# A two-layer Fourier metaformer on one core: the inverse width DFT folded into 64x64 quadrants, the mixed projection tile split into 64-row pairs, and five regimes with their own step orders and PSUM banks

## The chip, the core and the metric

The kernel runs on one NeuronCore of a Trainium2 chip. Its engines run side by side, each through its own queue in program order: TensorE (PE; its weight loads are PEld), VectorE (DVE), ScalarE (ACT), GpSimd (POOL) and SyncE (SP), which here issues all DMAs. The metric is the device time of one execution in microseconds, as the median of several.

## The reference

Eight images of 128 x 128 pixels with 96 channels go through two layers. Each layer is a spectral mixing block and a feed-forward block, both behind a layer norm and added to the residual. Cut to what matters:

```python
# conv block, per layer (x is the normed input, B, H, W, 96)
x_pre = scale * relu(einsum('bhwc,mc->bhwm', x, w1)) ** 2 + bias      # 192 channels
xf    = rfft2(x_pre)                                                 # over H and W
comb  = sum_s filt_s * r[b, s, m]     # three resized filters, weighted by a softmax gate per image
xsp   = irfft2(xf * comb)
y     = einsum('bhwm,cm->bhwc', xsp, w2)                              # back to 96 channels
# feed-forward block, in fp8-e5m2 operands with fp16 rounding of the sums
h = relu(q(x) @ q(W1) + q(b1)); y = q(h) @ q(W2) + q(b2)
```

The gate needs means over a whole image, and each Fourier transform mixes a whole row or column of it.

## The kernel before

The work is cut into three stages, each a Python generator whose `yield` ends a step, and each handles an image in 16 pieces:

- P, `pixels`, takes eight rows of pixels: 0 load xt, 1 norm statistics (DVE), 2 xn (POOL), 3 transposes pt_a (PE), 4 xT (ACT); then for j = 0 and 1: 5/10 projection pw (PE), 6/11 relu r (ACT), 7/12 square xs (ACT), 8/13 acc for the gate (POOL), 9/14 sum and difference sd (DVE); 15 width DFT pa (PE, in 64x64 quadrants), 16/18 lo (ACT), 17/19 at (DVE, L535 and L536), stored to the DRAM buffer a_d.
- F, `frequencies`, takes four width frequencies: 0 load al and ut, 1 ut times the gate (POOL, L626), 2 filter pf (PE, L639, 48-row halves), 3/7 height DFT py (PE, L673), 4 copies cf (ACT, L680), 5/8 products pr (DVE), 6/9 sums xf (POOL, L716), 10/12 projection pz (PE, L747 and L749), 11/13 zt (ACT, L757), 14 inverse height DFT pi (PE, L764), 15 yo (ACT), 16 yt (DVE), stored to y_d. The chunk k = 8 of an image is packed: it holds frequency 0 and 64 together, has a filter part px of its own (L655), adds a constant dc to al (DVE, L628) and clears parts of pr (POOL).
- S, `tokens`, takes eight rows: 0 load v and xr, 1 inverse width DFT ps_r (PE, L793), 2 add to xr (DVE, L802) and statistics, 3/4 norm to fp8 (halves of four rows; DVE L817 or ACT L811, by NORM_ACT), 5 transposes pt_c (PE), 6 xq (ACT, L828), then for k = 0 to 2: 7/11/15 pm (PE, L835), 8/12/16 y16 (ACT, L838), 9/13/17 a16 (DVE, L841), 10/14/18 cast to fp8 (ACT, or POOL in the tail), 19 po (PE), 20 o16 (ACT), 21 add b2 (DVE, L863), 22 residual sum y (POOL, L866) and store.
- N does the small arithmetic of both norms once a tick: 0 variance (DVE), 1 n_rs (ACT, L430 and L431), 2 a correction step and n_nb (DVE). G, the gate of an image, has eleven small steps, which the table GATE puts in front of certain places of TICK in the two ticks after the image's last piece of P.

The order of everything is written out by hand. Time runs in ticks t. In each tick the list TICK is walked, and an entry (stage, step, ahead) issues that step for piece t - offset + ahead. So a larger `ahead` issues a step earlier. F runs 19 ticks behind P and S 40 ticks behind P. Before, three lists are used: RAMP for t < 15 (P alone), TICK from 15 to 275, and TAIL from 276 on (S alone). For t from 15 to 37 S has nothing yet, and from 258 on P has ended, but TICK is used there too. With 16 images-and-layers of 16 pieces there are 256 pieces in each stage.

PSUM is held as four double banks d0 to d3. BANKS names the double bank of each tile, one buffer each: a tile waits until the tile before it on the same double bank has been read.

```python
def bank2(name):
    return pp.tile([128, 2, 512], F32, name=name, tag=f"d{banks[name]}")
```

The SBUF pool `ab` has two buffers for most tiles, three for v, xt and xf, five for xr.

Of the kernel before, what the change touches and what calls it, by code (L numbers as in the profile page):

```python
# [10 lines left out]
F32 = mybir.dt.float32  # L11
# [3 lines left out]
ALU = mybir.AluOpType  # L15
# [5 lines left out]
M = 2 * C  # L21
# [26 lines left out]
NORM_ACT, NORM_ACT_TAIL = (1,), (0, 1)  # L48
CAST_ACT, CAST_ACT_TAIL = (0, 1, 2), ()
XS_ACT = (0, 1)  # L50
# [75 lines left out]
def _constants():  # L126
# [33 lines left out]
    d[32] /= 2  # L160
    rh = np.concatenate([_resize_mat(h, H) for h, _ in SCALES], 1).T
# [35 lines left out]
def metaformer_kernel(ctx: ExitStack, tc: tile.TileContext, x, cst, layers, out):  # L197
# [8 lines left out]
    on_act = {}  # L206
# [61 lines left out]
    def prepare(us, l, p):  # L268
# [114 lines left out]
    def rows(ap, g):  # L383
        return ap.rearrange("w (s h) c -> w s h c", s=2)[:, :, g * RH : (g + 1) * RH, :]
# [7 lines left out]
    class Norms:  # L392
# [13 lines left out]
        def steps(self):  # L406
# [28 lines left out]
            tt(a, a, v, mult)  # L435
            if 1 in self.slots:
                nb = self.nb[:, 1]
                stt(nb, self.sm[:, 1, :, 0], -0.5, self.rs[:, 1], mult, mult)
                stt(nb, self.a[:, 1], 1.5, nb, add, mult)
            stt(rs, a, 1.5, rs, add, mult)  # L440
# [16 lines left out]
    def pixels(jb, g):  # L457
# [26 lines left out]
        for j in range(2):  # L484
# [10 lines left out]
            if j in XS_ACT:  # L495
                nc.scalar.activation(xs, r[:, :, :, :M], AF.Square)
            else:
                pv = pw.rearrange("p a (s c) -> p a s c", c=WE)
                nc.vector.tensor_tensor(xs, pv[:, :, :, :M], r[:, :, :, :M], ALU.mult)
# [9 lines left out]
            nc.vector.tensor_tensor(sd[:, 0], xs[:, 0], xs[:, 1], ALU.add)  # L509
            nc.vector.tensor_tensor(sd[:, 1], xs[:, 0], xs[:, 1], ALU.subtract)  # L510
# [99 lines left out]
    def frequencies(jb, k):  # L610
# [11 lines left out]
        nc.sync.dma_start(ut[:, :KC], ud[:, k0 : k0 + KC])  # L622
        if packed:
            nc.sync.dma_start(ut[:, KC:], ud[:, NKW - 1 :])
        yield
        nc.gpsimd.tensor_tensor(ut[:, :n], ut[:, :n], _bc_mid(jb.rw, n), ALU.mult)  # L626
# [6 lines left out]
        def filter_mm(j):  # L633
            pf = bank2(f"pf{j // 2}")
            for t in range(1 if packed and j == 0 else 0, 3):
                lo = 64 if packed and j == 0 and t == 1 else 0
                c0 = j * M + 128 * t
                for i in range(2):
                    mm(  # L639
                        pf[lo:, i, t * 128 : (t + 1) * 128],  # L640
                        utf[64 * i : 64 * i + NHS, c0 + lo : c0 + 128],
                        kt["rh"][64 * i : 64 * i + NHS, :],
                        start=True,
                        stop=True,
                    )
# [310 lines left out]
```

## Time and profile before

| | us |
|---|---|
| median of 3 runs | 5290.39 (5288.39 to 5291.29) |
| profiled execution, its own time | 5289.91 |
| span in the profile | 5288.1 |
| PE busy | 5025.9 (95%) |
| DVE busy | 4721.0 (89%) |
| ACT busy | 4404.8 (83%) |
| POOL busy | 2627.8 (50%) |
| DMA | 1020.45 MB, 193 GB/s over the span |

The span runs from the first to the last instruction, and the execution's own time is 1.8 us longer. Busy shares are averages over stretches with different limits. The profile can be cut into stretches of time, and the steps of a tick can be read from the timeline. Times in the text such as 3003.89 are us from the span's start. The distance from the start of one instruction to the start of the next on an engine that never idles is called its slot; durations are longer than slots[...].

### The profile page before, as it was taken

How to read it: one execution, taken by the hardware profiler on the slowest of the kernel's cores; microseconds unless marked ns; L12 is line 12 of the kernel's file. 1: busy time of each engine (PE TensorE's matmuls, PEld its weight loads, DVE VectorE, ACT ScalarE, POOL GpSimd, SP SyncE). 2: the span in 40 equal slices, each digit the busy share in tenths (PEclk: the TensorE clock that was granted, in tenths of full speed). 3: DMA queues.
4: the chain of work that ended last, by engine and by line, in shares of the span. 5: the costliest groups of instructions: out<-in, count | busy, mean ns of one | idle time of the engine just before them, and what ended most of it. 6: DMA issues, size and time to landing. Idle time of an engine off the chain costs nothing. (4 is left out here: it accounts for less than half of the span.)

```text
span 5288.1 us, 115779 instructions
## 1 busy us (share of the span) xinstructions
PE 5025.9 (95%) x41160; PEld 3997.8 (76%) x41160; DVE 4721.0 (89%) x13665; ACT 4404.8 (83%) x7147; POOL 2627.8 (50%) x1893
## 2 busy tenths in 40 slices
PE   4889999999999999999999999999999999998876
PEld 1677778788887878788787878878877878877753
DVE  3888889999998999999999999999999999999887
ACT  2745588888898888889898888988888888887778
POOL 0354545555555555555555555555555555554446
PEclk9999999999999999999999999999999999999988
DMA  5466677777777777777777777777777777776544
GB/s 147 162 157 158 169 195 204 205 201 207 205 209 199 204 203 203 204 205 209 201 205 205 206 200 204 211 199 205 205 203 205 206 208 205 198 201 169 165 145 130
DMA packets 908805, 1020.45 MB, mean 193 GB/s; under 512 B 67506, under 2 KB 840722, under 8 KB 907890
## 3 DMA queue, kind: packets, MB, share of 16 engines
q1 hardware_dynamic: 908228, 1013.04, 71.3%
q8 instruction: 327, 5.36, 0.4%
q14 instruction: 250, 2.05, 0.1%
HBM read 598.95 MB, written 413.84 MB: 192 GB/s over the span
## 5 line engine op out<-in xcount | busy, mean ns | idle before, releaser
L716 POOL TENSOR_TENSOR xf<-pr 128x768 f32<-128x768 f32 x512 | 954.8, 1865 | 778.5 <-DVE pr L701 719.8
L505 POOL TENSOR_TENSOR acc<-acc,r 128x192 f32<-128x192 f32 x496 | 338.0, 682 | 1233.3 <-ACT r L492 1224.5
L489 PE MATMUL pw<-w,xT 97*128 97x240 f32 x4096 | 926.1, 370 | 12.8 <-ACT xT L481 12.7
L489 PEld LDWEIGHTS pw<-w,xT 97*128 97x128 f32 x4096 | 763.2, 192 | 124.4 <-ACT xT L481 23.6
L673 PE MATMUL py<-k_fwd,al 128*128 128x128 f32 (+1 forms) x6208 | 832.6, 286 | 0.9
L838 ACT CAST y<-pm 128x1024 f16<-128x1024 f32 x768 | 774.4, 1009 | 41.0 <-PE pm L835 34.2
L673 PEld LDWEIGHTS py<-k_fwd,al 128*128 128x128 f32 (+1 forms) x6208 | 740.8, 194 | 48.4 <-issue 15.4
L845 ACT ACTIVATE h<-a 128x1024 fp8e5<-128x1024 f16 x706 | 747.0, 1058 | 4.7 <-DVE a L841 4.7
L697 DVE TENSOR_TENSOR pr<-py,cf 128x768 f32<-128x768 f32 x512 | 484.9, 947 | 254.4 <-PE py L673 237.0
L817 DVE TENSOR_SCALAR xn_c<-xr,n_rs,n_nb 128x96 fp8e5<-128x96 f32 x948 | 607.8, 700 | 0.0
L626 POOL TENSOR_TENSOR ut<-ut,rw 112x768 f32<-112x768 f32 (+1 forms) x256 | 473.7, 1850 | 242.3 <-DMA ut<-u_d 135.0
L492 ACT ACTIVATE r<-pw 128x960 f32<-128x960 f32 x512 | 492.3, 961 | 100.5 <-PE pw L489 98.5
L747 PE MATMUL pz<-w2b,xf 128*128 128x192 f32 x2048 | 541.8, 346 | 0.5 <-ACT rw L600 0.5
L835 PE MATMUL pm<-xq,f_q 96*128 96x512 fp8e5 x1536 | 465.6, 385 | 16.8 <-ACT zt L757 7.1
L757 ACT COPY zt<-pz 128x384 f32<-128x384 f32 x512 | 244.8, 478 | 271.5 <-PE pz L749 271.5
L747 PEld LDWEIGHTS pz<-w2b,xf 128*128 128x128 f32 x2048 | 329.7, 191 | 180.9 <-issue 142.8
L474 POOL TENSOR_TENSOR xn_a<-xt,n_rs 128x768 f32<-128x768 f32 x256 | 376.5, 1471 | 158.2 <-DMA xt<-in_x_dram 118.3
L639 PEld LDWEIGHTS pf<-k_rh,ut 48*128 48x128 f32 (+1 forms) x6080 | 365.3, 189 | 109.8 <-POOL xf L716 56.4
L793 PE MATMUL ps_r<-v,k_idft 128*128 128x384 f32 x1024 | 401.8, 516 | 41.9 <-DMA v<-y_d 18.2
L639 PE MATMUL pf<-k_rh,ut 48*128 48x128 f32 (+1 forms) x6080 | 419.5, 284 | 22.3 <-POOL ut L626 16.6
L841 DVE TENSOR_SCALAR a<-y,b 128x1024 f16<-128x1024 f16 x768 | 423.3, 551 | 15.2 <-ACT y L838 14.6
L866 POOL TENSOR_TENSOR y<-xr,o 128x768 f32<-128x768 f32 x256 | 425.6, 1662 | 21.7 <-ACT n_rs L431 11.4
(130 smaller groups left out, 10848.5 us busy)
## 6 DMA issues: line engine op xcount, KB each, us to landing
a_d<-at SPq DMA_DIRECT2D x256, 768.0 KB
al<-a_d SPq DMA_DIRECT2D x1024, 192.0 KB
y_d<-yt SPq DMA_DIRECT2D x512, 192.0 KB
v<-y_d SPq DMA_DIRECT2D x256, 384.0 KB
ut<-u_d SPq DMA_DIRECT2D x256, 336.0 KB
xt<-in_x_dram SPq DMA_DIRECT2D x512, 96.0 KB
xr<-in_x_dram SPq DMA_DIRECT2D x128, 384.0 KB
mid<-y SPq DMA_DIRECT2D x128, 384.0 KB
```

The source lines that it names most:

```text
L489: mm(o, xT[:, 4 * a + 2 * i + j, :], wt["w1"], start=True, stop=True)
L492: nc.scalar.activation(r.rearrange("p a s c -> p a (s c)"), pw, AF.Relu)
L626: nc.gpsimd.tensor_tensor(ut[:, :n], ut[:, :n], _bc_mid(jb.rw, n), ALU.mult)
L639: mm(pf[lo:, i, t * 128 : (t + 1) * 128], utf[64 * i : 64 * i + NHS, c0 + lo : c0 + 128], kt["rh"][64 * i : 64 * i + NHS, :], start=True, ...
L673: mm(py[p0:p1, t, e, :], alf[:, e, c0 + p0 : c0 + p1], f, start=True, stop=True)
L697: nc.vector.tensor_tensor(p0, yv, crb, ALU.mult)
L716: nc.gpsimd.tensor_tensor(xf.rearrange("p t e f -> p (t e) f"), pr[:, 0].rearrange("p t r k -> p t (r k)"), pr[:, 1].rearrange("p t r k -> ...
L747: mm(o[:, : 2 * C], xf[:, 1, e, :], wt["w2b"], start=True, stop=False)
L817: nc.vector.tensor_scalar(xn[:, j, :], x8[:, j, :], nm.rs[:, 1, j : j + 1], nm.nb[:, 1, j : j + 1], ALU.mult, ALU.add, saturate=False,)
L835: mm(pm[:, s, :], fk, xq[:, s, :], start=True, stop=True)
L838: nc.scalar.copy(y16, pm)
L845: nc.scalar.activation(hk, a16, AF.Copy, saturate=False)
```

## The change

- **Inverse width DFT.** The matrix `idft` is cut to its first 64 columns. Output pixels w and w + 64 differ only in the sign of the odd frequencies, so even (p = 0) and odd (p = 1) rows are multiplied apart, in four 64x64 quadrants, and VectorE adds both parts to the residual: one add of the even part over 768 elements, then an add and a subtract of the odd part over 384 each. Rows of the residual tiles are laid out anew, so the loads of xr and the stores of y are two DMAs each.
- **Mixed projection tile.** In pz the channel tile 1 holds 64 channels of each of two frequencies. It was multiplied by a 128 x 192 matrix padded with zeros; now its two 64-row halves are multiplied by their own 96 columns, side by side. All four frequencies go to one double bank `pz`, in two steps (the 64-row pairs, then the full tiles), and zt is copied once. F has 16 steps in place of 17: 10 and 11 are pz, 12 zt, 13 pi, 14 yo, 15 yt.
- **Regimes.** RAMP for t < 15, RISE for 15 to 37 (P and F), TICK for 38 to 257, FALL for 258 to 275 (F and S), TAIL from 276, each with its own order and banks. Loads are issued a tick earlier (P 0 ahead 4, F 0 and S 0 ahead 3), and ut is multiplied a tick earlier (F 1 ahead 2).
- **Smaller moves.** In the ramp the second of the two sd operations of each j goes to POOL; in the tail the add of b2 does, and the norm of six rows of eight is on ScalarE (before: all). One of the n_nb operations is gone. In `fft_mm` the loops are turned, and the packed chunk's extra frequency lies first in ut.

The core of the diff. A line of "..." stands for what is left out: the lists GATE, RISE_GATE and TAIL, the old lists, and the index changes of the packed chunk.

```diff
-NORM_ACT, NORM_ACT_TAIL = (1,), (0, 1)
+NORM_ACT, NORM_ACT_TAIL = (4, 5, 6, 7), (0, 1, 3, 4, 5, 7)
 CAST_ACT, CAST_ACT_TAIL = (0, 1, 2), ()
-XS_ACT = (0, 1)
+SD_POOL_RAMP = ((0, 1), (1, 1))
...
 TICK = (
...
+    ("S", 4, 0), ("S", 21, -2), ("P", 10, -1), ("P", 11, -1), ("P", 0, 4), ("F", 2, 1),
+    ("F", 3, 1), ("P", 2, 1), ("P", 1, 2), ("S", 5, 0), ("F", 4, 1), ("P", 12, -1),
+    ("S", 6, 0), ("S", 22, -2), ("S", 1, 1), ("F", 5, 1), ("S", 7, 0), ("S", 14, -1),
+    ("S", 2, 1), ("F", 9, 0), ("P", 3, 1), ("S", 8, 0), ("P", 13, -1), ("S", 15, -1),
+    ("P", 14, -1), ("S", 16, -1), ("N", 0, 0), ("S", 17, -1), ("P", 4, 1), ("S", 9, 0),
+    ("F", 6, 1), ("P", 5, 0), ("N", 1, 0), ("F", 10, 0), ("P", 15, -1), ("F", 11, 0),
+    ("P", 6, 0), ("N", 2, 0), ("F", 7, 1), ("P", 16, -1), ("P", 17, -1), ("P", 18, -1),
+    ("S", 10, 0), ("F", 12, 0), ("S", 0, 3), ("P", 19, -1), ("F", 13, 0), ("S", 11, 0),
+    ("S", 18, -1), ("P", 7, 0), ("F", 8, 1), ("F", 14, 0), ("S", 12, 0), ("P", 8, 0),
+    ("F", 0, 3), ("F", 1, 2), ("F", 15, 0), ("S", 19, -1), ("S", 13, 0), ("S", 3, 1),
+    ("S", 20, -1), ("P", 9, 0),
 )
...
+RISE = (
+    ("P", 1, 2), ("F", 3, 1), ("N", 0, 0), ("F", 4, 1), ("P", 3, 1), ("P", 5, 0),
+    ("F", 10, 0), ("P", 14, -1), ("P", 15, -1), ("P", 0, 3), ("P", 4, 1), ("P", 6, 0),
+    ("F", 5, 1), ("F", 11, 0), ("N", 1, 0), ("P", 16, -1), ("P", 17, -1), ("P", 7, 0),
+    ("P", 8, 0), ("F", 6, 1), ("F", 7, 1), ("F", 1, 2), ("P", 18, -1), ("P", 19, -1),
+    ("F", 12, 0), ("F", 8, 1), ("P", 9, 0), ("N", 2, 0), ("P", 10, 0), ("P", 2, 2),
+    ("P", 11, 0), ("F", 13, 0), ("F", 14, 0), ("F", 0, 3), ("P", 12, 0), ("F", 2, 2),
+    ("F", 15, 0), ("P", 13, 0), ("F", 9, 1),
+)
...
+FALL = (
+    ("S", 14, -1), ("F", 1, 1), ("F", 2, 1), ("F", 3, 1), ("F", 4, 1), ("S", 1, 1),
+    ("S", 21, -3), ("S", 22, -3), ("S", 15, -1), ("S", 4, 0), ("S", 5, 0), ("S", 6, 0),
+    ("F", 9, 0), ("F", 5, 1), ("S", 2, 1), ("F", 6, 1), ("F", 7, 1), ("S", 7, 0),
+    ("S", 8, 0), ("S", 16, -1), ("S", 9, 0), ("F", 10, 0), ("F", 11, 0), ("S", 10, 0),
+    ("F", 12, 0), ("S", 11, 0), ("N", 0, 0), ("S", 17, -1), ("S", 18, -1), ("F", 13, 0),
+    ("S", 19, -1), ("N", 1, 0), ("F", 8, 1), ("N", 2, 0), ("S", 12, 0), ("F", 14, 0),
+    ("S", 13, 0), ("F", 15, 0), ("F", 0, 3), ("S", 3, 1), ("S", 0, 3), ("S", 20, -1),
+)
 RAMP = (
...
+    ("P", 17, -1), ("N", 1, -1), ("P", 2, 2), ("P", 0, 4), ("P", 3, 2), ("P", 18, -1),
+    ("P", 19, -1), ("P", 6, 1), ("P", 12, 0), ("P", 7, 1), ("P", 4, 2), ("P", 1, 4),
+    ("N", 2, -1), ("P", 8, 1), ("P", 13, 0), ("P", 14, 0), ("N", 0, 0), ("P", 9, 1),
+    ("P", 10, 1), ("P", 15, 0), ("P", 11, 1), ("P", 16, 0), ("P", 5, 2),
 )
...
 BANKS = {
...
+    "ps_g": 0, "ph": 1, "pl": 3, "pa0": 2, "pa1": 3, "pw0": 1, "pw1": 1, "pt_a": 3,
+    "pf0": 3, "pf1": 2, "py0": 0, "py1": 1, "pz": 0, "pi": 2, "ps_r": 2, "pt_c": 1,
+    "pm0": 1, "pm1": 3, "pm2": 0, "po": 0, "px": 1, "pg": 0,
+}
...
+    d = d[:, :HH]
...
             stt(a, rs, -0.5, rs, mult, mult)
             tt(a, a, v, mult)
+            stt(rs, a, 1.5, rs, add, mult)
             if 1 in self.slots:
                 nb = self.nb[:, 1]
                 stt(nb, self.sm[:, 1, :, 0], -0.5, self.rs[:, 1], mult, mult)
-                stt(nb, self.a[:, 1], 1.5, nb, add, mult)
-            stt(rs, a, 1.5, rs, add, mult)
...
-            nc.vector.tensor_tensor(sd[:, 0], xs[:, 0], xs[:, 1], ALU.add)
-            nc.vector.tensor_tensor(sd[:, 1], xs[:, 0], xs[:, 1], ALU.subtract)
+            for e, op in enumerate((ALU.add, ALU.subtract)):
+                on = nc.gpsimd if (j, e) in on_pool["sd"] else nc.vector
+                on.tensor_tensor(sd[:, e], xs[:, 0], xs[:, 1], op)
...
-        zt = ab.tile([128, 2, KC * C], F32, name="zt")
-        for j, xf in zip((0, 2), xfs):
-            pz = bank2(f"pz{j // 2}")
+        pz = bank2("pz")[:, :, : 4 * C].rearrange("p t (j e c) -> p t j e c", j=2, e=2)
+        for j, xf in enumerate(xfs):
             for e in range(2):
-                o = pz[:, e, :]
-                mm(o[:, : 2 * C], xf[:, 1, e, :], wt["w2b"], start=True, stop=False)
+                for t in range(2):
+                    q = slice(64 * t, 64 * t + 64)
+                    mm(
+                        pz[:, t, j, e, :], xf[q, 1, e, :], wt["w2b"][q],
+                        start=j == e == 0, stop=False,
+                    )
+        yield
+        for j, xf in enumerate(xfs):
+            for e in range(2):
                 for t in range(2):
                     mm(
-                        o[:, t * C : (t + 1) * C],
-                        xf[:, 2 * t, e, :],
-                        wt["w2c" if t else "w2a"],
-                        start=False,
-                        stop=t == 1,
+                        pz[:, t, j, e, :], xf[:, 2 * t, e, :], wt["w2c" if t else "w2a"],
+                        start=False, stop=j == e == 1,
                     )
...
-        pr = bank2("ps_r")
         for s in range(2):
-            mm(
-                pr[:, s, : RH * C].rearrange("p (h c) -> p h c", c=C),
-                kt["idft"],
-                v[:, :, s, :],
-                start=True,
-                stop=True,
-            )
-        yield
-        xv = xr.rearrange("p s h c -> p s (h c)")
-        nc.vector.tensor_tensor(xv, pr[:, :, : RH * C], xv, ALU.add)
+            nc.sync.dma_start(xr[64 * s : 64 * s + 64], rows(jb.src, g, s))
+        yield
+        pr = bank2("ps_r")[:, :, : RH * C]
+        for p in range(2):
+            for s in range(2):
+                q = slice(64 * p, 64 * p + 64)
+                mm(
+                    pr[64 * s : 64 * s + 64, p].rearrange("p (h c) -> p h c", c=C),
+                    kt["idft"][q],
+                    v[q, :, s, :],
+                    start=True,
+                    stop=True,
+                )
+        yield
+        xv = xr.rearrange("p a h c -> p a (h c)")
+        nc.vector.tensor_tensor(xv, _bc_mid(pr[:, 0], 2), xv, ALU.add)
+        for a, op in enumerate((ALU.add, ALU.subtract)):
+            nc.vector.tensor_tensor(xv[:, a], xv[:, a], pr[:, 1], op)
...
-                if h in on_act["norm"]:
+                if j in on_act["norm"]:
...
-        nc.vector.tensor_tensor(o16, o16, _bc_mid(wt["b2"], RG), ALU.add)
+        on = nc.gpsimd if on_pool["b2"] else nc.vector
+        on.tensor_tensor(o16, o16, _bc_mid(wt["b2"], RG), ALU.add)
...
-        nc.sync.dma_start(rows(jb.dst, g), y)
+        for s in range(2):
+            nc.sync.dma_start(rows(jb.dst, g, s), y[64 * s : 64 * s + 64])
...
             if t < offset["F"] - 4:
-                order, places = RAMP, RAMP_BANKS
-            elif t > n + offset["F"]:
-                order, places = TAIL, TAIL_BANKS
+                order, places, late_steps = RAMP, RAMP_BANKS, {}
+            elif t < offset["S"] - 2:
+                order, places, late_steps = RISE, RISE_BANKS, RISE_GATE
+                on_pool.update(sd=())
+            elif t < n + 2:
+                order, places, late_steps = TICK, BANKS, GATE
+            elif t <= n + offset["F"]:
+                order, places, late_steps = FALL, FALL_BANKS, {}
+            else:
+                order, places, late_steps = TAIL, TAIL_BANKS, {}
                 on_act.update(norm=NORM_ACT_TAIL, cast=CAST_ACT_TAIL)
-            else:
-                order, places = TICK, BANKS
+                on_pool.update(b2=True)
```

## The prediction

> **What bounds the kernel now.** I read the page's first line and engine shares, then the stretches by regime, then the timeline of one steady tick, then single groups.
>
> ```profile
> span 5288.1 us, 115779 instructions
> PE 5025.9 (95%) x41160; PEld 3997.8 (76%) x41160; DVE 4721.0 (89%) x13665; ACT 4404.8 (83%) x7147; POOL 2627.8 (50%) x1893
> ```
>
> ```profile
> 123.00:239.00 116.00, 100.25 (x633) 74.19 (x632) 98.76 (x380) 88.24 (x162) 42.98 (x49) 1.00 0.44 150
> 239.00:611.00 372.00, 330.58 (x2475) 273.18 (x2474) 310.01 (x716) 185.58 (x325) 178.19 (x130) 0.95 0.62 158
> 611.00:4835.00 4224.00, 4189.63 (x35089) 3379.67 (x35089) 3889.18 (x11391) 3750.90 (x5980) 2180.06 (x1557) 0.99 0.76 203
> 4835.00:5126.00 291.00, 243.97 (x1961) 190.66 (x1958) 258.07 (x635) 213.70 (x345) 120.02 (x71) 0.94 0.57 158
> 5126.00:5288.00 162.00, 109.77 (x805) 63.67 (x804) 121.34 (x402) 141.56 (x274) 101.06 (x79) 0.86 0.41 132
> ```
>
> Columns: span, then busy us of PE, PEld, DVE, ACT, POOL, and PE's clock, the DMA share and GB/s. The third row, some 220 ticks with all three stages, has PE busy 99%: there PE's stream is the tick. In rows 2 and 4 (22 ticks without S, 18 without P) PE has 11% and 16% idle, so those ticks (372/22 = 16.9 us, 291/18 = 16.2 us) are set by the order of steps. One steady tick on PE:
>
> ```profile
> 3000.91 1.61 PE L639 MATMUL pf<-k_rh,ut 48*128 48x128 f32 x24
> 3002.45 1.60 PE L673 MATMUL py<-k_fwd,al 128*128 128x128 f32 x12
> 3003.89 0.61 PE L825 MATMUL pt_c<-ident,xn_c 128*96 128x128 fp8e5 x8
> 3004.34 1.51 PE L793 MATMUL ps_r<-v,k_idft 128*128 128x384 f32 x4
> 3005.68 0.60 PE L835 MATMUL pm<-xq,f_q 96*128 96x512 fp8e5 x2
> ...
> 3008.94 1.79 PE L489 MATMUL pw<-w,xT 97*128 97x240 f32 x8
> 3010.66 1.52 PE L519 MATMUL pa<-sd,dft 64*64 64x384 f32 x16
> 3012.11 0.59 PE L747 MATMUL pz<-w2b,xf 128*128 128x192 f32 x2
> ...
> 3019.62 1.61 PE L639 MATMUL pf<-k_rh,ut 48*128 48x128 f32 x24
> ```
>
> Start to start gives slots, and pf to pf the tick: **18.71 us**. Each f32 matmul is two records. ps_r: 4 records, 1.34 us. pa: sixteen 64x64 records with the same 384 columns, 1.45 us, so four quadrants run side by side (about 0.32 us a round of four). VectorE and ScalarE:
>
> ```profile
> L817 DVE TENSOR_SCALAR xn_c<-xr,n_rs,n_nb x728: 314/318/1824, 1213.9 to 4690.5; 128x96 fp8e5<-128x96 f32 x182
> 3003.01 1.48 ACT L680 COPY cf<-pf 128x768 f32<-128x768 f32 x2
> 3004.54 1.02 ACT L828 ACTIVATE xq<-pt_c 96x1024 fp8e5<-96x1024 f32 x1
> 3005.46 0.83 ACT L496 ACTIVATE xs<-r 128x768 f32<-128x768 f32 x1
> ```
>
> L817 has a median of 318 ns and a maximum of 1824. Four in a tick need some 1.0 us and take 2.5: 1.5 us of VectorE is waiting inside them.
>
> [...] in the single records the last pw, with a slot of 0.202, starts at 3010.364, pa at 3010.658, 0.09 us late; the first record after pa has its weight load uncovered, 0.1 us more. [...] 48 rows (pf) 189 ns, 128 rows (py) 194. So 64-row halves cost as many loads, but pf shows them in pairs, 0.112 us a pair. [...] L817: its maximum is one xf of POOL (L716, 1.82 to 1.92 us).
>
> **The change, part by part**, for a steady tick.
>
> *PE.* ps_r goes from 1.35 to two rounds of 0.32, 0.05 for its loads and a drain of 0.09 on either side: 0.88, **-0.47**. pz takes 3.13 us now (1.51 + 1.62). After: eight pairs at 0.112 + 0.1 for the first load + 0.09 drain = 1.08, then sixteen records at 0.1115 (the py pace[...]) + 0.1 = 1.88; 2.96, -0.17. One drain ahead of pz is new, +0.09. PE's sum becomes **18.2 us**, 0.55 under today's tick.
>
> *VectorE.* One add of 0.87 (L802) becomes three: 0.98 with the wait for its own result, 0.47, 0.58: +1.05. One n_nb operation goes (-0.09). L817 gets clean: in the new order POOL has done ut and xn_a when L817 comes, and its y waits for the add of b2 behind L817: -1.5. Sum 16.7 us; now 17.2 (92% of 18.71).
>
> *ScalarE.* Nothing added; its slots make 17.0 us. It had 1.5 us of idle per tick, at 18.2 it has 1.2.
>
> *SP.* xr and y become two DMAs each, 17 issues a tick for 15, loads (P0, S0, F0) a tick earlier. DMA is at 0.76 and SP's queue mostly waits for yt and at (1467 and 877 us), so I take nothing; without that cover, each late load is a PE wait at pf, py or ps_r.
>
> *The new order.* I laid the steps of one tick on the engines with these slots, T = 0 at the end of po. PE: pw1 1.78, pf to 3.32, py0, pt_c and ps_r to 6.09, then pm0. pm0 needs xq. ScalarE: cf can start when pf's last result is there, 3.43; cf 0.68 + 0.69, xs1 0.73 stand ahead of xq in its queue: xq runs 5.53 to 6.55, pm0 starts at 6.60. **PE waits 0.5 us.** From there PE: pm0, pt_a, pm2 1.75, a wait of 0.1 for the bank of pm0 (d1), pw0 1.71, pz 1.08, pa 1.45, pz's rest 1.88, py1 1.34, pi 1.35, pm1 0.44, po 1.02: 12.1. **Tick 18.73.** The gain of PE is given back to a wait on ScalarE. Next in line is VectorE: pr0 can start at 4.9 (py0), three adds, stats and sd1 follow, N0 ends at 11.9; ScalarE's n_rs (N1) stands there from 10.6 on, and behind it r0, lo, a cast and zt, which is still 0.2 us early for pi. Against 18.713, over 206 plain ticks: **+4 us**.
>
> *Per image.* The mean interval of xT (L481) is 19.18, so an image pays 7.5 us beside its 16 x 18.71: the packed chunk and the gate. The dc add (L628, 1166 ns, waiting for POOL) moves to a tick ahead and the gate is spread anew; the px part gets longer in the ScalarE chain (+0.6). I take -1.5 x 13.75 images = **-20** (bounds -50, +15).
>
> *RISE.* Without S, PE's slots are py 2.78, pt_a 0.88, pw 3.4, pz 2.96, pa 1.45, pi 1.36, pf 1.64: 14.5; VectorE 11, ScalarE 8. I find no wait between engines as long as the 0.5 above. 22 x 14.5 + 9 for two gates and a packed chunk = 328 for 372: **-43** (bounds -55, -15).
>
> *FALL.* Slots: PE 12.6, ScalarE 11.8, VectorE 12. Laid out, pf1 waits for po's copy: 13.7, with L817 blocked now and then 14.5, for 16.2: **-30** (bounds -45, 0).
>
> *RAMP.* VectorE 6.4 us of 6.81; two subtractions (0.47 each) go to POOL (4.4 us): about 6.1, x 15: **-10** (bounds -14, +5[...]). *TAIL.* ScalarE 7.5 of some 7.5 to 9; two of eight norms (0.36) go to VectorE, b2 to POOL, v is asked for earlier; but VectorE has +1.05[...]: **-8** (bounds -25, +20).
>
> Sum: +4 - 20 - 43 - 30 - 10 - 8 = **-107**. Profiled execution 5289.91 (0.5 under the median of 5290.39): **5183**.
>
> **Rivals.**
> A, PE stays full. If cf, xs and xq are faster to reach pm0 than I laid out, the tick is 18.2: 206 x -0.55 = -113 more, 5070. For it: today's order leaves PE 1% idle. Against: the 0.5 us wait comes from four durations in a row. 0.2.
> B, VectorE binds, slower. POOL's ut or xn_a falls on L817 again (place: S3, end of the tick). Price: 1.5 us on VectorE, of which 0.7 is free ahead of pr0; 0.8 passes through the three adds, N0 and N1 to zt, 0.2 is slack there: tick 19.35, +130, 5315. It decides from about 1.4 us of blocking a tick on, where +0.5 x 206 eats the 107. For it: 1.5 us today. Against: POOL's queue, with y behind b2. 0.11.
> C, the regimes give little: early ticks are bound by loads or by PE's clock (0.95 in row 2, 0.94 in row 4). RISE and FALL -20 in place of -73: 5236. 0.17.
> D, the quadrants of ps_r do not run side by side: two rounds more, +0.65 us, x 206 = +134: 5317. pa, the same form, speaks against it: 0.02.
> My forecast has 0.5.
>
> **How the numbers follow.** A measurement can tell 0.2% (10.6 us). Forecast, with +-0.25 us on the tick (+-52 us): 5130 to 5240. A lies below, C at its upper end, B and D slower. To leave out 0.2 (half of A, B and D) and to take in the bounds of the parts: **5080 to 5290**. Faster 0.82 (A, the forecast, 0.12 of C), same 0.05 (the rest of C), slower 0.13 (B, D).
>
> **What would show it.** Right: PE busy in the steady row falls to 96 to 97% with pm waiting for xq, L817 at one duration near 318, ps_r near 0.1 us a record, RISE ticks near 14.5. Wrong: steady xT interval under 18.4 (A), L817 still to 1.8 us and ScalarE's n_rs waiting over 2 us (B), pz pairs slower than 0.112.

## The result and the profile after

The changed kernel takes **5158.38 us** (median of 4 runs, 5151.53 to 5159.17) against 5289.39 for the kernel before beside it; ratio 0.9753, 95% interval 0.9736 to 0.977. The profiled execution took 5158.86 us:

```profile
span 5156.8 us, 123945 instructions
PE 4888.7 (95%) x44232; PEld 3746.4 (73%) x44232; DVE 4532.4 (88%) x13904; ACT 4359.2 (85%) x7108; POOL 2608.7 (51%) x1947
```

The shares lie within two points of those before; PE has shed 137 us. The stretches by regime (span, busy us of PE, PEld, DVE, ACT, POOL, PE's clock, DMA share, GB/s) say more:

```profile
121.00:236.70 115.70, 101.36 (x649) 72.06 (x649) 105.95 (x362) 88.81 (x162) 85.46 (x80) 1.00 0.45 153
236.70:551.00 314.30, 305.65 (x2606) 252.02 (x2606) 262.69 (x708) 181.04 (x324) 166.82 (x129) 0.98 0.67 189
551.00:4721.00 4170.00, 4079.31 (x37749) 3171.26 (x37748) 3753.74 (x11616) 3724.20 (x5982) 2101.34 (x1558) 1.00 0.74 206
4721.00:4964.00 243.00, 219.71 (x2102) 165.86 (x2103) 201.26 (x608) 199.52 (x321) 112.54 (x66) 0.97 0.70 183
4964.00:5156.00 192.00, 131.35 (x938) 68.91 (x930) 166.38 (x481) 140.78 (x258) 137.72 (x106) 0.68 0.39 115
```

In the third row PE is 98% busy, not 99%: it waits a little in each tick. In the second it is 97%, where it was 89%. To put the change into parts I took the same marks in both traces: the starts of the same xT pieces (ScalarE, once a tick in P) and yo pieces (once a tick in F), and subtracted.

| stretch, from mark to mark | before | after | change | predicted |
|---|---|---|---|---|
| start and RAMP, to xT piece 17 | 239.25 | 236.74 | -2.5 | -10 |
| RISE, to xT piece 39 | 371.90 | 314.28 | -57.6 | -43 |
| TICK, to yo piece 239 | 4225.45 | 4169.78 | -55.7 | -16 (+4 - 20) |
| FALL, to yo piece 255 | 261.31 | 229.69 | -31.6 | -30 |
| TAIL, to the end | 190.19 | 206.31 | +16.1 | -8 |
| sum | | | -131.3 | -107 |

The plain tick went from 18.713 to 18.638 us. Its PE timeline, where the prediction expected the new wait:

```profile
3002.66 0.61 PE L866 MATMUL pt_c<-ident,xn_c 128*96 128x128 fp8e5 x8
3003.20 0.88 PE L832 MATMUL ps_r<-v,k_idft 64*64 64x384 f32 x8
3004.38 0.59 PE L876 MATMUL pm<-xq,f_q 96*128 96x512 fp8e5 x2 [0.30 <-ACT xq L869]
3004.81 1.04 PE L511 MATMUL pt_a<-ident,xn_a 128*96 128x128 f32 x8
...
3008.05 1.14 PE L776 MATMUL pz<-w2b,xf 64*128 64x96 f32 x16
```

ps_r's slot is 0.88 (1.34 before), and PE then stands 0.30 us for xq. The waits of the steady stretch, PE's first (total us, times, longest), then ScalarE's:

```profile
PE pm L876 <- ACT xq L869: 62.6, 180, 0.8
```

```profile
ACT n_rs L464 <- DVE n_v L462: 268.0, 180, 3.7
```

PE waits 0.35 us a tick for xq; ScalarE stands 1.5 us a tick at n_rs for VectorE. L817 (now L858), which had 314/318/1824 ns, is clean:

```profile
L858 DVE TENSOR_SCALAR xn_c<-xr,n_rs,n_nb x700: 315/322/329, 1202.3 to 4493.0; 128x96 fp8e5<-128x96 f32 x175
```

### The profile page after: what moved, and what is told of

Same layout as the page of the kernel before. It is cut to its first block, busy times and chain, and to the rows that moved or that the text cites. A ratio compares the mean times of both kernels' runs of the same rounds, so it can differ in the third digit from the quotient of the medians.

```text
span 5156.8 us, 123945 instructions
## 1 busy us (share of the span) xinstructions
PE 4888.7 (95%) x44232; PEld 3746.4 (73%) x44232; DVE 4532.4 (88%) x13904; ACT 4359.2 (85%) x7108; POOL 2608.7 (51%) x1947
## 5 line engine op out<-in xcount | busy, mean ns | idle before, releaser
L522 PE MATMUL pw<-w,xT 97*128 97x240 f32 x4096 | 957.6, 377 | 4.2 <-DVE pr L730 2.1
L534 POOL TENSOR_TENSOR acc<-acc,r 128x192 f32<-128x192 f32 x496 | 296.6, 598 | 987.3 <-ACT r L525 928.1
L540 DVE TENSOR_TENSOR sd<-xs 128x384 f32<-128x384 f32 x993 | 508.9, 552 | 4.2 <-ACT xs L528 3.5
L528 ACT ACTIVATE xs<-r 128x768 f32<-128x768 f32 x512 | 438.0, 859 | 0.1
L852 ACT ACTIVATE xn_c<-xr,n_nb,n_rs 128x96 fp8e5<-128x96 f32 x1061 | 407.9, 459 | 31.8 <-DVE n_nb L473 31.8
L668 PEld LDWEIGHTS pf<-k_rh,ut 48*128 48x128 f32 x6080 | 361.7, 188 | 86.2 <-issue 78.5
L668 PE MATMUL pf<-k_rh,ut 48*128 48x128 f32 x6080 | 413.5, 282 | 5.0 <-POOL ut L656 1.8
L784 PE MATMUL pz<-w2a,xf 128*128 128x96 f32 x2048 | 418.1, 286 | 0.0
L784 PEld LDWEIGHTS pz<-w2a,xf 128*128 128x128 f32 x2048 | 312.1, 192 | 144.3 <-issue 142.8
L549 PE MATMUL pa<-sd,dft 64*64 64x384 f32 x4096 | 392.5, 496 | 7.1 <-ACT xT L514 4.5
```

Source lines behind the costliest of these rows:

```text
L522: mm(o, xT[:, 4 * a + 2 * i + j, :], wt["w1"], start=True, stop=True)
L540: on.tensor_tensor(sd[:, e], xs[:, 0], xs[:, 1], op)
L668: mm(pf[:, i, t * 128 : (t + 1) * 128], utf[64 * i : 64 * i + NHS, c0 : c0 + 128], kt["rh"][64 * i : 64 * i + NHS, :], start=True, stop=True,)
L784: mm(pz[:, t, j, e, :], xf[:, 2 * t, e, :], wt["w2c" if t else "w2a"], start=False, stop=j == e == 1,)
```

## Experiments

All edits start from the changed kernel unless it says otherwise. Ratios are to the kernel before, run beside each on the same chip, where it took 5298.74 to 5302.34 us; a tick is the median xT interval in the steady stretch. A digit behind a step's name is its j or k: xs1 is the square of j = 1, y0 the copy y16 of k = 0.

### What the fold is worth

**old_ps_r** puts the unfolded inverse width DFT back; the rest of the change stays.

```diff
-        for p in range(2):
-            for s in range(2):
-                q = slice(64 * p, 64 * p + 64)
...
+        for s in range(2):
...
+                kt["idft"],
+                v[:, :, s, :],
...
-        nc.vector.tensor_tensor(xv, _bc_mid(pr[:, 0], 2), xv, ALU.add)
-        for a, op in enumerate((ALU.add, ALU.subtract)):
-            nc.vector.tensor_tensor(xv[:, a], xv[:, a], pr[:, 1], op)
+        nc.vector.tensor_tensor(xv, pr[:, :, : RH * C], xv, ALU.add)
```

> Changed kernel with the old inverse width DFT (one 128-row matrix, one add of 768, one DMA each for xr and y), all else as changed. Theory: PE's extra 0.47 us fills the wait of pm for xq and the rest of the drains; plain tick 18.65 to 18.75, total 0 to +25 us on the changed kernel: within this order the fold saves almost nothing. Rival (PE's sum sets the tick): 19.1, +100 us.

Measured 5144.19 us, ratio 0.9707 (0.9692 to 0.9721): **faster than the changed kernel**, where the theory had a loss of 0 to 25 us. Its plain tick is 18.635, against 18.638. PE is full for once (second number of the row):

```profile
1300.00:4600.00 3300.00, 3293.40 (x29329) 2590.30 (x29329) 2825.94 (x8909) 3007.09 (x4769) 1674.61 (x1247) 1.00 0.69 207
```

The changed kernel has PE at 3235 us in the same window. So the fold takes 0.33 us of work from PE in each tick (58 us over 177 ticks; ps_r's slot is 0.46 shorter, the slot of pt_c ahead of it 0.09 longer, 0.54 for 0.45, the 0.09 that the prediction calls a drain), and all of it comes back as waiting. Without the fold PE's stream alone is the tick, and it lies 0.08 under the 18.713 of before. That is as much as the prediction gives the pz pairs (-0.17 + 0.09), but no run here undoes the pairs alone. The fold also costs outside the plain ticks: the TAIL tick is 8.58 without it and 8.83 with it.

**fold_alone** is the kernel before with only the fold (matrix, quadrants, adds, DMAs), in the old order and banks. Of its diff, the adds:

```diff
...
-        nc.vector.tensor_tensor(xv, pr[:, :, : RH * C], xv, ALU.add)
+        nc.vector.tensor_tensor(xv, _bc_mid(pr[:, 0], 2), xv, ALU.add)
+        for a, op in enumerate((ALU.add, ALU.subtract)):
+            nc.vector.tensor_tensor(xv[:, a], xv[:, a], pr[:, 1], op)
```

> Kernel before with the folded inverse width DFT alone (64x64 quadrants, three adds, two DMAs each for xr and y), old order and banks. Theory: PE reaches pm 0.47 us earlier, but xq is ready only 0.07 us before pm's present start, so PE waits; VectorE gets 1.05 us more beside L817 still blocked by POOL (17.2 + 1.05 of 18.71): plain tick 18.6 to 19.1, total -20 to +90 us on the kernel before. Rival (PE's sum sets the tick): 18.24, -100 us.

Measured 5589.17 us, ratio 1.0547 (1.0529 to 1.0566), tick 20.37. Both expectations fell; the loss is over three times the larger one. VectorE's timeline in a steady tick, then POOL's:

```profile
3006.79 2.10 DVE L848 TENSOR_SCALAR a<-y,b 128x1024 f16<-128x1024 f16 x1
...
3012.86 2.54 DVE L824 TENSOR_SCALAR xn_c<-xr,n_rs,n_nb 128x96 fp8e5<-128x96 f32 x4
```

```profile
3006.80 1.81 POOL L628 TENSOR_TENSOR ut<-ut,rw 112x768 f32<-112x768 f32 x1
...
3012.69 1.92 POOL L718 TENSOR_TENSOR xf<-pr 128x768 f32<-128x768 f32 x1 [2.47 <-DVE pr L703]
```

a16 takes 2.10 us for 0.47 while POOL does ut, and the four norms 2.54 for 1.04 while it does xf (the norms were blocked as long before). VectorE is busy 3197 of 3300 us: with 0.93 us more of adds (1.91 from the first add to the statistics, for 0.98) and about 3 us of blocked time it is the bound, and PE also waits for its adds, since ps_r and pm0 share a bank in the old table:

```profile
PE pm L842 <- DVE xr L809: 150.0, 167, 1.3
```

So the new TICK order is what makes the fold affordable; the fold makes neither order faster.

**xq_early** moves pt_c, xq and y0 forward in TICK so that pm0 need not wait.

```diff
-    ("F", 3, 1), ("P", 2, 1), ("P", 1, 2), ("S", 5, 0), ("F", 4, 1), ("P", 12, -1),
-    ("S", 6, 0), ("S", 22, -2), ("S", 1, 1), ("F", 5, 1), ("S", 7, 0), ("S", 14, -1),
-    ("S", 2, 1), ("F", 9, 0), ("P", 3, 1), ("S", 8, 0), ("P", 13, -1), ("S", 15, -1),
+    ("S", 5, 0), ("F", 3, 1), ("P", 2, 1), ("P", 1, 2), ("F", 4, 1), ("S", 6, 0),
+    ("P", 12, -1), ("S", 22, -2), ("S", 1, 1), ("F", 5, 1), ("S", 7, 0), ("S", 8, 0),
+    ("S", 14, -1), ("S", 2, 1), ("F", 9, 0), ("P", 3, 1), ("P", 13, -1), ("S", 15, -1),
```

> Changed kernel with three moves in TICK: pt_c (S5) ahead of py0 (F3), xq (S6) ahead of xs1 (P12), y16 of k=0 (S8) ahead of the cast (S14). Theory (two chains): the wait of pm for xq (0.35 us a tick) and of pw0 for y16 (0.1) go, but py0 and with it pr0, the adds, sd1 and N0 come 0.45 us later; n_rs, r0, lo, cast and zt stand behind N0, so pi waits 0.7 us for zt: plain tick 18.9 in place of 18.64, total +50 us on the changed kernel. Rival (the wait at pm is all that PE loses): tick 18.2, total -95 us.

Measured 5249.19 us, ratio 0.9905 (0.9888 to 0.9922), tick 19.06: the theory's direction, with a larger loss than its 18.9. PE does not wait for xq any more; it waits at pi instead:

```profile
PE pi L800 <- ACT zt L791: 63.9, 143, 0.7
```

Two chains hold the tick: cf, xs1, xq to pm0, and py0, the adds, statistics, N0 and n_rs to zt and pi. Shortening the first lengthens the second, since py0 now stands behind pt_c.

**xq_early_r0** is xq_early with r0 ahead of n_rs on ScalarE besides, to fill the wait there.

```diff
-    ("F", 6, 1), ("P", 5, 0), ("N", 1, 0), ("F", 10, 0), ("P", 15, -1), ("F", 11, 0),
-    ("P", 6, 0), ("N", 2, 0), ("F", 7, 1), ("P", 16, -1), ("P", 17, -1), ("P", 18, -1),
+    ("F", 6, 1), ("P", 5, 0), ("P", 6, 0), ("N", 1, 0), ("F", 10, 0), ("P", 15, -1),
+    ("F", 11, 0), ("N", 2, 0), ("F", 7, 1), ("P", 16, -1), ("P", 17, -1), ("P", 18, -1),
```

> The same three moves, and relu r0 (P6) ahead of n_rs (N1) in ScalarE's queue, so that 0.85 us of work no longer stands behind the wait for N0. Theory (two chains): zt is then early enough for pi, PE runs with hardly a wait: plain tick 18.2 (18.15 to 18.35), total -90 us on the changed kernel, 5065 to 5075. Rival (one chain only): no difference between this run and the one without the r0 move.

Measured 5466.27 us, ratio 1.0315 (1.0299 to 1.033), tick 20.06; the theory fell, and so did the rival, which had no difference to xq_early. Two of the five small operations of N0 in VectorE's timeline, and POOL's:

```profile
3016.97 0.50 DVE L460 SCALAR_TENSOR_TENSOR n_v<-n_d 128x16 f32<-128x16 f32 x1
3017.50 1.74 DVE L461 SCALAR_TENSOR_TENSOR n_v<-n_sm,n_v 128x16 f32<-128x16 f32 x1
```

```profile
3016.84 0.59 POOL L534 TENSOR_TENSOR acc<-acc,r 128x192 f32<-128x192 f32 x1 [2.27 <-ACT r L525]
3017.38 1.82 POOL L656 TENSOR_TENSOR ut<-ut,rw 112x768 f32<-112x768 f32 x1
```

r0 releases POOL's acc, and ut follows at once. Both fall on N0, and an operation of 16 elements a partition, 0.17 us when clean, takes 1.74. zt then comes 1.5 us late at pi (200.2 us over 134 ticks).

**xq_early_n0** and **xq_early_n0_zt** start from xq_early and shorten the second chain as well. The diff is that of the first; the second has ("F", 12, 0) ahead of ("P", 6, 0).

```diff
-    ("P", 14, -1), ("S", 16, -1), ("N", 0, 0), ("S", 17, -1), ("P", 4, 1), ("S", 9, 0),
-    ("F", 6, 1), ("P", 5, 0), ("N", 1, 0), ("F", 10, 0), ("P", 15, -1), ("F", 11, 0),
-    ("P", 6, 0), ("N", 2, 0), ("F", 7, 1), ("P", 16, -1), ("P", 17, -1), ("P", 18, -1),
-    ("S", 10, 0), ("F", 12, 0), ("S", 0, 3), ("P", 19, -1), ("F", 13, 0), ("S", 11, 0),
+    ("N", 0, 0), ("S", 16, -1), ("P", 14, -1), ("P", 4, 1), ("N", 1, 0), ("N", 2, 0),
+    ("F", 6, 1), ("P", 5, 0), ("S", 17, -1), ("S", 9, 0), ("F", 10, 0), ("F", 11, 0),
+    ("P", 15, -1), ("P", 6, 0), ("F", 12, 0), ("F", 7, 1), ("P", 16, -1), ("P", 17, -1), ("P", 18, -1),
+    ("S", 10, 0), ("S", 0, 3), ("P", 19, -1), ("F", 13, 0), ("S", 11, 0),
```

> The changed kernel with pt_c, xq and pm0 earlier as in xq_early, and besides: N0 ahead of sd1 on VectorE, n_rs and N2 right behind, pz's rest ahead of pa on PE, zt ahead of lo on ScalarE. Theory (two chains hold the tick, PE waits for xq in the one and ScalarE waits for n_v, then PE for zt, in the other; shorten both and PE's stream of 18.2 us is the tick): plain tick 18.2 to 18.35, some -60 to -90 us on the changed kernel. Rival (r0 comes earlier as N1 does, POOL's acc0 and ut follow at once and fall on the small VectorE operations N2 and on sd1, which are blocked up to 1.8 us as n_v was in xq_early_r0): tick 18.6 to 19.5, 0 to +180 us.

> As xq_early_n0 but with zt ahead of r0 on ScalarE, so that POOL's acc0 and ut start some 0.8 us later, behind N2 and sd1; ScalarE idles some 0.75 us more ahead of zt. Theory of the two chains: tick 18.2 to 18.4 and no blocked n_ operation; -50 to -90 us on the changed kernel. Rival (ScalarE with 16.9 us of work and over 1.3 us of waits becomes the tick): 18.6 to 19.0, 0 to +75 us.

Measured 5461.66 (1.0317, 1.0292 to 1.0343; tick 19.78) and 5248.33 (0.9912, 0.9888 to 0.9936; tick 18.92). Both theories (18.2 to 18.4) fell. In the first the rival came true on another operation, and with a longer tick than it said: not N2 or sd1 but a16, two of them in 2.78 us for 0.88, beside POOL's acc and ut; in this tick pi then waits 1.22 us. VectorE's timeline:

```profile
3000.65 2.78 DVE L882 TENSOR_SCALAR a<-y,b 128x1024 f16<-128x1024 f16 x2
```

In the second nothing is blocked, the tick is the rival's (18.6 to 19.0), and a plain tick has one wait of PE left, 0.37 us at py1 for r0.

**xq_early_banks** takes that wait away by exchanging banks in xq_early_n0_zt.

```diff
-    "ps_g": 0, "ph": 1, "pl": 3, "pa0": 2, "pa1": 3, "pw0": 1, "pw1": 1, "pt_a": 3,
-    "pf0": 3, "pf1": 2, "py0": 0, "py1": 1, "pz": 0, "pi": 2, "ps_r": 2, "pt_c": 1,
-    "pm0": 1, "pm1": 3, "pm2": 0, "po": 0, "px": 1, "pg": 0,
+    "ps_g": 0, "ph": 1, "pl": 3, "pa0": 2, "pa1": 3, "pw0": 1, "pw1": 0, "pt_a": 3,
+    "pf0": 3, "pf1": 2, "py0": 0, "py1": 0, "pz": 0, "pi": 2, "ps_r": 2, "pt_c": 1,
+    "pm0": 1, "pm1": 3, "pm2": 0, "po": 1, "px": 1, "pg": 0,
```

> xq_early_n0_zt with three banks exchanged (py1 and pw1 from bank 1 to 0, po from 0 to 1), so that py1 does not wait for r0 any more. Theory (the wait of 0.37 us at py1 is the only one left on PE, whose slots there add up to 18.55): plain tick 18.55 to 18.65, some 55 to 75 us less than xq_early_n0_zt, level with the changed kernel or up to 20 us under it. Rival (ScalarE, with 16.9 us of work and 2.1 of waits, is the cycle: the wait goes to another place): 18.85 to 19.0, no change on xq_early_n0_zt.

Measured 5343.12 us, ratio 1.0087 (1.0068 to 1.0106). The plain tick stays 18.92, the rival's value: PE now waits 0.36 us at pi for VectorE's `at`, behind it ScalarE's waits of 0.97 at n_rs and 0.75 at zt. The 95 us over xq_early_n0_zt, which neither theory nor rival had, lie in the gate ticks: the two of an image cost 11.4 us beside plain ticks, for 4.6.

### What the regimes are worth

**regimes_off** uses RISE only until F's first piece, and FALL only for the last two ticks.

```diff
-            elif t < offset["S"] - 2:
+            elif t < offset["F"] + 1:
...
-            elif t < n + 2:
+            elif t < n + offset["F"] - 1:
```

> The changed kernel with RISE used only for its first ticks (until the first plane is ready for frequencies) and FALL only for the last two ticks before TAIL; all ticks in between follow TICK. Theory (the regimes' own orders are worth what the ledger shows, some 58 us in the rise and 32 in the fall, of which the common TICK order with its idle stage left out gives a part back): +60 to +85 us on the changed kernel, rise ticks 16.5 to 18, fall ticks 15.5 to 16.5. Rival (an idle stage makes the ticks short in any order, the gain comes from elsewhere): less than +20 us.

Measured 5230.26 us, ratio 0.988 (0.9856 to 0.9903): 67 us more by the profiled spans. Rise ticks are 15.9 for 14.32, and the stretch to xT piece 39 ends 35.6 us later; fall ticks are 15.5 to 18.1 for 14.14, and FALL takes 36.7 more. The theory holds in the sum; rise ticks are shorter than its 16.5 to 18, and some fall ticks longer than its 15.5 to 16.5. TICK with an idle stage is still about a microsecond a tick faster in the rise than the old TICK was, but no faster in FALL (266.4 us for 261.3).

**ramp_tail_on_vectore** gives the ramp's two subtractions and the tail's b2 back to VectorE.

```diff
-SD_POOL_RAMP = ((0, 1), (1, 1))
+SD_POOL_RAMP = ()
...
-                on_pool.update(b2=True)
+                on_pool.update(b2=False)
```

> The changed kernel with the two subtractions of RAMP (SD_POOL_RAMP) and the adds of b2 in TAIL given back from POOL to VectorE; nothing else differs. Theory ([...]what POOL takes over it takes from VectorE's time too): TAIL tick 8.83 to some 8.0 us, n_a (L468, L469) back from 999 and 946 ns to some 170, RAMP tick within -0.5 to +0.2 us; in all -10 to -25 us on the changed kernel. Rival (VectorE is the busy engine there and POOL relieves it): TAIL tick 9.2 to 9.5 us, +7 to +20 us.

Measured 5176.35 us, ratio 0.9779 (0.9752 to 0.9806). My theory fell for both: the ramp tick is 7.86 for 6.86, the TAIL tick 9.30 for 8.83, the rival's figure. In the new orders POOL's help is needed.

**old_ps_r_old_tail** is old_ps_r with the kernel before's TAIL (order, banks, all norms on ScalarE, b2 on VectorE). The two lists are those of the kernel before; beside them:

```diff
-NORM_ACT, NORM_ACT_TAIL = (4, 5, 6, 7), (0, 1, 3, 4, 5, 7)
+NORM_ACT, NORM_ACT_TAIL = (4, 5, 6, 7), (0, 1, 2, 3, 4, 5, 6, 7)
...
-                on_pool.update(b2=True)
+                on_pool.update(b2=False)
```

> old_ps_r (the changed kernel with the unfolded inverse width DFT and one add) with the kernel before's TAIL besides: its step order and banks, all eight norms on ScalarE, b2 on VectorE. Theory (of the 16 us that the tail lost, some 6 are the fold's adds, which old_ps_r gives back, and some 10 come from the new tail order with its norms and b2): the stretch behind the last yo piece 255 falls from 200 us in old_ps_r to 188 to 192, the whole run by 8 to 12 us. Rival (the new tail order is no worse and the loss sits in the hand-over from FALL): 198 to 206 us, no gain or a loss of some 5.

Measured **5128.83** us (5126.85 to 5130.04), ratio 0.9683 (0.9662 to 0.9704): the fastest of all. Behind yo piece 255 it takes 186.4 us, 13.8 less than old_ps_r (200.2), and more than the 8 to 12 of the theory. The loss of 16.1 in TAIL is thus 6.1 for the fold (206.3 - 200.2) and 13.8 for the new tail order with its norms and b2, less 3.8 that comes from elsewhere (190.2 - 186.4). The old tail is the shorter one with the fold too: fold_alone, which has both, takes 201.7 us there, the changed kernel 206.3.

**old_ramp_pool_sd** adds the old RAMP order and banks to that, with the subtractions still on POOL. Its first lines:

```diff
 RAMP = (
-    ("P", 17, -1), ("N", 1, -1), ("P", 2, 2), ("P", 0, 4), ("P", 3, 2), ("P", 18, -1),
+    ("P", 5, 1), ("P", 17, -1), ("P", 18, -1), ("P", 2, 2), ("P", 11, 0), ("N", 1, -1),
...
 RAMP_BANKS = {
-    "pa0": 1, "pa1": 0, "pw0": 3, "pw1": 2, "pt_a": 1,
+    "pa0": 1, "pa1": 3, "pw0": 2, "pw1": 0, "pt_a": 0,
```

> old_ps_r_old_tail with the kernel before's RAMP order and banks besides, but the two subtractions still on POOL. The kernel before has 6.81 us a ramp tick, the changed one 6.86, and the changed one with the subtractions on VectorE 7.86. Theory (what POOL takes over, VectorE gains, as the prediction said; the new order costs what POOL brings): 6.0 to 6.3 us a tick, -8 to -13 us on old_ps_r_old_tail. Rival (1380 ns of POOL and the VectorE operations that it excludes are as long a chain in any order): 6.7 to 7.3 us, -2 to +8 us.

Measured 5158.3 us, ratio 0.974 (0.972 to 0.976). Ramp ticks are 8.1 and 9.4 to 9.8: both expectations fell. POOL does both subtractions behind acc, PE's pa waits for them (14.1 us over 10 ticks), and three of N0's operations are blocked (0.37, 0.85 and 0.92 us, for 0.17). The relief exists only in an order that was laid out for it, and that order with it only equals the old one without it.

### Where an image's 3 us come from

With the xT intervals averaged by their place in the image, an image paid 7.3 us beside plain ticks before (gate 2.9 + 0.2, packed tick 4.1, 0.1 behind it) and pays 4.3 now (1.8 + 0.5, 1.9, 0.1). So 2.2 of the 3 us come from the packed tick and 0.8 from the gate. The old packed tick on PE:

```profile
2522.08 1.26 PE L655 MATMUL px<-k_rh,ut 112*128 112x128 f32 x8 [1.70 <-DVE yt L771]
2523.28 3.51 PE L673 MATMUL py<-k_fwd,al 128*128 128x128 f32 x16
2526.58 0.94 PE L825 MATMUL pt_c<-ident,xn_c 128*96 128x128 fp8e5 x8
2527.36 1.51 PE L793 MATMUL ps_r<-v,k_idft 128*128 128x384 f32 x4
```

px waits for VectorE's yt (they share d2), and in this image py and pt_c then run at a lower clock: pt_c takes 0.94 for 0.61, and the clock of the tick is 0.93, where it is 1.00 in the packed tick of 22.0 us from 1896.80. That is why old packed ticks are 21.6 to 22.0 in some images and 23.7 to 26.2 in others. In the new banks px waits 0.17 us, and all packed ticks but one (20.6) are 20.5.

**gate_old_places** puts the gate's steps at the old places in the new TICK.

```diff
-    1: ((26, 0), (44, 1), (52, 2), (53, 3), (55, 4), (59, 5), (61, 6)),
-    2: ((23, 7), (35, 8), (41, 9), (48, 10)),
+    1: ((42, 0), (42, 1), (45, 2), (49, 3), (52, 4), (57, 5), (61, 6)),
+    2: ((0, 7), (20, 8), (29, 9), (32, 10)),
```

> The changed kernel with the gate's steps at the places of the kernel before (42 to 62, here 61 as the list is one shorter, then 0, 20, 29, 32) in TICK; nothing else differs. Theory (the gain of 3.2 us an image comes for the most part from spreading the gate's chain): an image pays 6 to 8 us beside its plain ticks, for 4.3, +20 to +50 us on the changed kernel. Rival (it comes from the order around it, the dc add clear of POOL and the packed chunk's shape): 4 to 5 us an image, within 10 us of the changed kernel.

Measured 5301.62 us, ratio 1.0003 (0.9996 to 1.0011): ten moved table entries cost as much as the **whole** change gains. An image pays 15.3 us, over twice what the theory said, while packed ticks stay at 20.5. Yet the theory's reading, that most of an image's gain comes from spreading the gate, is not shown: the same numbers stood for other places in the old list, where the gate cost 3.1 us and not the 13.3 of this run. PE's timeline of two gate ticks:

```profile
1690.09 0.25 PE L587 MATMUL ph<-gsum,fc1g 96*68 96x1 f32 x2 [1.23 <-DVE pr L730]
...
1691.24 1.15 PE L600 MATMUL pl<-hm,fc 68*96 68x1 f32 x12 [0.78 <-DVE hm L594]
...
1693.50 3.30 PE L522 MATMUL pw<-w,xT 97*128 97x240 f32 x8
...
1706.02 0.35 PE L627 MATMUL pg<-ident,rwT 96*112 96x96 f32 x2 [2.69 <-DVE rwT L622]
1706.20 3.01 PE L522 MATMUL pw<-w,xT 97*128 97x240 f32 x8
1709.14 2.03 PE L776 MATMUL pz<-w2b,xf 64*128 64x96 f32 x16
```

PE waits 2.0 and 2.7 us for the gate's chain through VectorE, and after each wait eight pw records take 3.30 and 3.01 us for 1.85, the pz pairs 2.03 for 1.14. The clock of those two ticks (third number from the end), against a plain one in the last row:

```profile
1680.20:1704.30 24.10, 20.81 (x185) 16.08 (x183) 18.74 (x62) 17.25 (x30) 9.34 (x7) 0.93 0.66 191
1704.30:1729.00 24.70, 22.68 (x177) 17.13 (x178) 17.69 (x58) 17.68 (x29) 9.54 (x7) 0.86 0.43 124
1729.00:1747.60 18.60, 18.30 (x172) 14.21 (x171) 16.88 (x54) 16.91 (x28) 9.56 (x7) 1.00 0.83 225
```

Length times (1 - clock), summed over the gate ticks of 14 images, gives 94 of the 142 us that this kernel lost, an estimate; before it was 12, in three images of 14, and in the changed kernel 0. PE's waits at ph, pl and pg are 51 us in 11 images, 4.6 each of the 11 that an image loses. By this estimate the larger part of a late gate is not the wait but the clock behind it.

In these traces the granted clock changes between 1.00 and 0.50 on a grid of 3.41 us. The window before such a fall was not idle from end to end. Cut on this grid, the same ticks read (PE's busy time is the second number, its clock the third from the end):

```profile
1689.60:1693.01 3.41, 2.14 (x34) 2.12 (x35) 2.78 (x10) 0.31 (x1) 0.00 (x0) 1.00 0.40 153
1693.01:1696.42 3.41, 3.41 (x18) 2.97 (x15) 3.37 (x15) 2.33 (x6) 1.21 (x1) 0.50 0.99 237
...
1703.25:1706.66 3.41, 0.71 (x6) 0.65 (x6) 3.34 (x17) 2.28 (x4) 0.60 (x1) 1.00 0.41 120
1706.66:1710.08 3.42, 3.42 (x15) 2.57 (x15) 2.27 (x12) 1.27 (x4) 0.00 (x0) 0.50 0.00 0
```

Most of the 2.14 us, some 1.4, are the one-column matmuls of ph and pl. In the kernel before, px's wait of 1.44 us that ends at 1910.25 falls across a line of the grid (1909.45; PE busy 2.77 and 2.61 us in the two windows) and the clock stays at 1.00, while the 1.11 us that end at 3134.61 lie in one window (PE busy 2.31 of 3.42) and the next one, from 3134.84, is at 0.50. In these two cases the time for which PE stood within one window told them apart, and not the length of the wait. A fixed limit does not come out of these traces: the window at 588.50 had PE busy for 1.70 us and the clock stayed at 1.00.

## Why the prediction was right or wrong

- **The plain tick: mechanism right, size near.** PE's slots with the fold, the wait of pm for xq, and "the gain is given back" are all in the trace. The wait is 0.35 for 0.5, and the tick 18.638 for 18.73, so +4 was really some -15 (0.075 x 206); PE is busy 98%, where 96 to 97 was to show it. VectorE's adds came to +0.93: the prediction's three parts make +1.16 on the 0.87 that it names, and its +1.05 only on a slot of 0.98. xq_early and its four followers show the other half, that VectorE's chain to n_rs and zt stands close behind; old_ps_r shows the price: the fold is worth nothing in TICK.
- **Per image: mis-sized.** -1.5 was -3.05, for 13.75 images -42 in place of -20, inside the bounds. The term left out px's wait for yt (18.8 us in 14 steady images before, 1.3 each) and the clock that follows waits of PE (length times 1 - clock is some 1.2 us in a steady packed tick before, an estimate). The dc add is off its POOL wait as expected (302 ns for 1166).
- **RISE: right, low.** Ticks of 14.32 for 14.5, and -57.6 for -43. The first three ticks are short (36 us, where three of 14.5 make 43.5); the packed chunk costs 2.2 and the one gate in full ticks 2.5, where I allowed 9 for them and a second gate. (The term's own sum, 328 for 372, is -44.) PE's wait of pt_a for VectorE's pr, 31.5 us in 19 ticks before, is gone, and the clock rose from 0.95 to 0.98.
- **FALL: right in size**, -31.6 for -30 (ticks of 14.14 for 14.5), and in part by luck: L858 is not blocked there (at most 328 ns), and pf's weights wait for po's copy only 0.3 us a tick; PE stands 0.5 at pi for zt and 0.4 at py for pr, waits that the layout did not name.
- **RAMP: wrong step.** "Two subtractions go to POOL: about 6.1" took 0.94 us off VectorE and put nothing back. The ramp tick is 6.86 us, for 6.81 before; the -2.5 of the table comes from the start (xT piece 2 begins 3.5 us earlier), not from the ramp ticks. In the new trace VectorE is busier in the same window (81.6 of 85 us, 78.8 before), and a small operation beside a subtraction on POOL lasts longer: n_sm takes 0.97 us, where it takes 0.18 in the new tail (5029.45). VectorE's timeline, then POOL's:

```profile
169.30 0.97 DVE L458 TENSOR_TENSOR n_sm<-st 128x16 f32<-128x16 f32 x1
170.19 0.16 DVE L459 TENSOR_TENSOR n_d<-st 128x8 f32<-128x8 f32 x1
```

```profile
168.85 1.39 POOL L540 TENSOR_TENSOR sd<-xs 128x384 f32<-128x384 f32 x1
```

  n_sm ends at 170.27, POOL's operation at 170.24. The prediction had room for a loss only in its bound of +5.
- **TAIL: wrong sign.** +16.1 for -8, inside the bounds (-25, +20). VectorE's +1.05 was seen and still set against gains that did not come. In the steady part of the old tail ScalarE was the fullest engine (115.6 of 124 us, VectorE 100.7); in the new one it is VectorE (135.7 of 140, ScalarE 111.6), with the adds, the two norms and what POOL blocks (n_a 1.00 and 0.94 us, where the n_rs and n_nb behind it take 0.17). PE's clock is lower there too, 0.70 for 0.89; what that costs is not shown. N2 in the new tail, on VectorE, then POOL:

```profile
5031.03 1.00 DVE L468 SCALAR_TENSOR_TENSOR n_a<-n_rs 128x8 f32<-128x8 f32 x1
5032.06 0.94 DVE L469 TENSOR_TENSOR n_a<-n_a,n_v 128x8 f32<-128x8 f32 x1
```

```profile
5030.79 2.21 POOL L888 CAST h<-a 128x1024 fp8e5<-128x1024 f16 x2 [1.43 <-DVE a L882]
```

- **The sum: near, in part by luck.** RAMP and TAIL came out 31.6 us worse than their terms, TICK, RISE and FALL 55.9 better; -107 is close to -131 because these errors cancel in part.
- **Rivals.** A (tick 18.2) did not come: the tick without pm's wait would be 18.3, and every order that took that wait away was slower. B (VectorE blocked by POOL) did not occur in the changed kernel, but it is what happened in fold_alone, xq_early_r0 and xq_early_n0, on other operations than L817 as well, at the size that B gave it or more. C is refuted by the ledger (RISE and FALL -89) and regimes_off, D by ps_r's slot of 0.88.

Open: whether an order exists in which PE's 18.3 us with the fold is the tick. Five orders were tried, none was below 18.638.

## What to carry to other kernels

Work taken from the busiest engine is worth nothing if the work that it causes elsewhere lies on the chain that feeds that engine (here the fold's 0.33 us a tick came back as waiting); undo that one part inside the finished kernel to see its worth, not only alone in the old one. Price a wait of TensorE with the slower clock that can follow it (some 94 of the 142 us that gate_old_places lost, an estimate), and look at where short serial chains such as a gate make TensorE wait (the gate cost 13.3 us an image there, 2.3 in the changed kernel). When an operation moves to GpSimd, list the VectorE operations that will run beside it: in these traces some lasted about to the end of GpSimd's operation, which weighs most for the short ones (0.17 us became 0.94 to 1.74).

## What was not expected of the hardware

- PE's clock fell after windows of 3.41 us in which PE stood for as little as 1.1 us (before, ahead of 3134.84), or did matmuls of one column for some 1.4 us and stood 1.27 (gate_old_places, ahead of 1693.01); the next one or two windows, 3.4 to 6.8 us, ran at a clock of 0.50 in these cases.
- VectorE operations of 8 or 16 elements a partition took 0.94 to 1.74 us beside a GpSimd operation, for 0.17 (n_sm and n_a in the changed kernel, n_v in xq_early_r0), and lasted about to the end of GpSimd's operation (n_v to 3019.24, ut to 3019.20). The fp16 a16, a tensor_scalar of 128x1024, is blocked too: 2.10 us for 0.47 in fold_alone.
- A subtraction of 128x384 takes 0.55 us on VectorE. On GpSimd it takes 1.38 in the changed ramp, where VectorE starts the other one of the pair at the same time, and a median of 1.00 in old_ramp_pool_sd, where it does not; so some 0.4 of the 1.38 is GpSimd's own waiting, an estimate from the two. The ramp's term had GpSimd at 4.4 us a tick; it was busy for 5.4.
